# Routed rows fetched as quarter rows and turned by VectorE's block transposes

## Chip, core and metric

The kernel runs on one core of one Trainium2 chip. The metric is the device time of one execution in microseconds (us). Before the change the median of three runs is 294.49 us (294.01 to 295.79).

## What is computed

The input is `x`, 625 rows of 1024 features in float32, with 20000 edges of two types. A graph layer comes first, then a mixture-of-experts layer. Cut to what matters here:

```
g  = x + layernorm(x) + elu(rgcn(t5_norm(layernorm(x)))) @ wo      # graph layer with residual
xf = layernorm(g)                                                  # 625 x 1024, "h2" in the kernel
shared = mean over 2 shared experts of gelu(xf @ sW1 + sb1) @ sW2 + sb2
gates  = xf @ rW + rb                                              # 8 experts
w      = softmax of the two largest gates, zero elsewhere
h_e    = gelu(xf @ W1[e] + b1[e])                                  # 1024 -> 256
moe    = sum over e of w[:, e] * (h_e @ W2[e] + b2[e])             # 256 -> 1024
out = g + xf + shared + moe                                        # residuals as in the reference
```

## The kernel before

The kernel does not run every expert over every row. It routes: each of the 625 rows has two experts, so there are 1250 (row, expert) pairs, and they are packed into 11 tiles of 128 slots (`NJ = 11`). Seven tiles belong wholly to one expert (numbers 4 to 10), three are split into two halves of different experts (0 to 2) and one is split into four quarters (3). The order in which they are worked on is 4, 5, 6, 0, 7, 1, 8, 2, 9, 10, 3.

The stages around the change are these.

- **The normalized rows.** `output_proj` (L976) computes `h2` for each 125-row block, stores it to DRAM as `h2d` from the GpSimd queue (L993), and `to_columns` puts its transpose into `h2T`.
- **Loads.** The SyncE queue loads `w1a` (the eight `W1`, 8 MB, L1078), `sw1` and `w2a` (the eight `W2`, 8 MB, L1109). `w1a` is laid out so that partition p holds the features p, 128 + p, 256 + p and so on.
- **Routing.** `gate` and `route` compute the gates and weights. `slots` (L1188) works out on VectorE, in many small instructions, which slot each pair gets. A matrix product `p_tok` (L1288) turns this into one row number per slot. L1294 makes from it `tok`, the row to gather for each of the 128 x 11 slots; `row` (L1296) says where the result of a slot goes.
- **Shared experts.** `shared_in` (L1170, `p_sh`) runs before, between and after these steps and keeps TensorE filled.
- **Bias rows.** `bias_parts` fetches `b2x` with three DMAs from the GpSimd queue (L641) into a buffer of the pool `io`, which has three buffers; VectorE reads it last at L645 (`b2h`).
- **First half of the routed experts.** For each tile, `fetch` (L1368) gathers the 128 rows with one indirect DMA from the GpSimd queue (L1370) into an `io` buffer `xs`. TensorE transposes them in eight 128 x 128 blocks (L1378, `p_x`). ScalarE copies one half of the result to `xsT` (L1384), VectorE the other (L1382). `xsT` has two buffers. `expert_in` (L1393, `p_h`, L1397) multiplies `xsT` with `w1a`, and VectorE copies the result to `hj` (L1401). `expert_mid` (L1406) transposes `hj` and applies the gelu on ScalarE (L1412, `hjT`). For the halves and quarters of the split tiles ScalarE also copies pieces of `w1a` to `w1m` (L1391). The loop runs the three steps for neighbouring tiles: fetch of step s, `expert_in` of s - 1, `expert_mid` of s - 2.
- **Second half and end.** `p_yj` (L1455) multiplies `hjT` with `w2a`; the rows are scattered to `yt` (L1463), read back as `g` (L1474) and added to `x1` with the shared experts' second product `p_o` (L1510, L1512); the result is stored.

[...] The GpSimd queue of this stage holds, in this order, the three `b2x` DMAs, the eleven gathers and the eleven scatters.

Of the kernel before, what the change touches and what calls it, by code (L numbers as in the profile page):

```python
# [8 lines left out]
F32 = mybir.dt.float32  # L9
F16 = mybir.dt.float16  # L10
BF16 = mybir.dt.bfloat16
F32R = mybir.dt.float32r
I32 = mybir.dt.int32
I16 = mybir.dt.int16
AF = mybir.ActivationFunctionType
ALU = mybir.AluOpType
AX = mybir.AxisListType

N = 625
D = 1024  # L20
# [6 lines left out]
TP = 125  # L27
NT = N // TP
KD = D // 128
# [13 lines left out]
QC = 32  # L43
NJ = 11
# [409 lines left out]
def sparse_kernel(  # L454
# [24 lines left out]
    nc = tc.nc  # L479

    def pool(stack, name, bufs=1, side="left", **kw):
        return stack.enter_context(tc.tile_pool(name=name, bufs=bufs, side=side,
                                                reuse_waits="tile", **kw))

    const = pool(ctx, "const")
# [4 lines left out]
    h2d = dram.tile([N, D], F32, name="h2d")  # L490
# [4 lines left out]
    def ps_acc(name):  # L495
        return psum[0].tile([128, 512], F32, tag="acc", name=name, bufs=nacc[0])

    def ps_mm(name):
        return psum[0].tile([128, 512], F32, tag="mm", name=name, bufs=3)
# [64 lines left out]
    ident = const.tile([128, 128], F32, name="ident")  # L564
# [61 lines left out]
    for i in (2, 3):  # L626
# [5 lines left out]
                                               ap=[[0, 3], [D, NS], [1, D]]))  # L632
    nc.gpsimd.dma_start(bd[:, NS:, :], bass.AP(tensor=b2.tensor, offset=b2.offset,
                                               ap=[[0, 3], [D, NE], [1, D]]))
    b23 = const.tile([3 * QC, D], BF16, name="b23")

    def bias_parts():
# [5 lines left out]
        for j in range(3):  # L643
# [3 lines left out]
            if j < 2:  # L647
# [13 lines left out]
                                    ap=[[0, 4], [D, QC], [1, D]]))  # L661
# [87 lines left out]
    vT = const.tile([128, NV], F32, name="vT")  # L749
# [324 lines left out]
    w1a = pool(in_w, "w1a", side="right").tile([128, NE, KD, H], F32, name="w1a")  # L1074

    def load_w1(es):
        for e in es:
            nc.sync.dma_start(w1a[:, e], W1[e].rearrange("(k p) h -> p k h", p=128))  # L1078

    load_w1(range(2))  # L1080
    sh_in = ExitStack()
    for s in range(NT + 2):
        if s == 0:
# [4 lines left out]
            rt = pool(sh_in, "rt", side="right")  # L1088
# [17 lines left out]
    io = pool(ctx, "io", 3)  # L1106
# [33 lines left out]
    def route():  # L1140
        full = [TP, NT, NE, NE]
        other = gates[:, :, None, :].to_broadcast(full)
        own = gates[:, :, :, None].to_broadcast(full)
        nc.vector.tensor_scalar(lower, lower, 0.0, None, op0=ALU.is_gt)
        above = rt.tile(full, F32, name="above")
        equal = rt.tile(full, F32, name="equal")
        nc.vector.tensor_tensor(above, other, own, op=ALU.is_gt)
        nc.vector.tensor_tensor(equal, other, own, op=ALU.is_equal)
        nc.vector.tensor_mul(equal, equal, lower[:, None, :, :].to_broadcast(full))
        nc.vector.tensor_add(above, above, equal)  # L1150
        cnt = const.tile(wide, F32, name="cnt")
        nc.vector.tensor_reduce(cnt, above, axis=AX.X, op=ALU.add)
        nc.vector.tensor_scalar(sel, cnt, 1.5, None, op0=ALU.is_lt)
        top = const.tile([TP, NT], F32, name="top")
        nc.vector.tensor_reduce(top, gates, axis=AX.X, op=ALU.max)
        ex = const.tile(wide, F32, name="ex")
        nc.vector.tensor_sub(ex, gates, top[:, :, None].to_broadcast(wide))
        nc.scalar.activation(ex, ex, AF.Exp)
        nc.vector.tensor_mul(ex, ex, sel)
        tot = const.tile([TP, NT], F32, name="tot")  # L1160
        nc.vector.tensor_reduce(tot, ex, axis=AX.X, op=ALU.add)
        inv = const.tile([TP, NT], F32, name="tot_inv")
        nc.vector.reciprocal(inv, tot)
        nc.vector.memset(w[:, :, :NS], 1.0)
        nc.vector.tensor_mul(w[:, :, NS:], ex, inv[:, :, None].to_broadcast(wide))


    shT = hid.tile([128, NS, HK, N], F32, name="shT")

    def shared_in(i, t):  # L1170
        b = KD + i * HK + t
        for a, z in CUTS:
            p = ps_acc(f"p_sh_{i}_{t}_{a}")
            for k in range(KD):
                nc.tensor.matmul(p[:, : z - a], sw1[:, i, k, t * 128 : (t + 1) * 128],  # L1175
                                 h2T[:, k, a:z], start=(k == 0), stop=(k == KD - 1))
            nc.scalar.activation(shT[:, i, t, a:z], p[:, : z - a], AF.Gelu, bias=vT[:, b : b + 1])

    wab = const.tile([TP, 2, NT], F32, name="wab")
    tok = const.tile([128, NJ], I32, name="tok")
    row = const.tile([128, NJ], I32, name="row")
    ej = const.tile([1, nt + 4], I32, name="ej")

    def slots():  # L1188
        nc.vector.tensor_scalar(below, below, 0.0, None, op0=ALU.is_gt)
        ones = const.tile([TP, TP], F16, name="ones")  # L1190
        nc.vector.memset(ones, 1.0)
        p = ps_mm("p_rank")
        rank = p[:TP, : NT * NE].rearrange("p (t e) -> p t e", t=NT)
        shared_in(0, 0)
        nc.tensor.matmul(p[:TP, : NT * NE], below, sel.rearrange("p t e -> p (t e)"),
                         start=True, stop=False)
        for t in range(NT - 1):
            nc.tensor.matmul(rank[:, t + 1 :, :], ones,
                             sel[:, t][:, None, :].to_broadcast([TP, NT - 1 - t, NE]),
                             start=False, stop=(t == NT - 2))  # L1200
# [37 lines left out]
        for i in range(2):  # L1238
# [6 lines left out]
                                       op0=ALU.is_ge, op1=ALU.mult)  # L1245
# [12 lines left out]
        full = const.tile([TP, 2, NT], I32, name="full")  # L1258
# [27 lines left out]
        for a in range(2):  # L1286
            for t in range(NT):
                nc.tensor.matmul(q[:, :NJ], oh[:, a, t], oj[:, a, t],  # L1288
                                 start=(a == 0 and t == 0), stop=(a == 1 and t == NT - 1))

        t = rt.tile([128, 2, NJ], F32, name="t")
        nc.vector.tensor_scalar(t[:, 0], q[:, :NJ], float(YB), float(YB), op0=ALU.is_ge, op1=ALU.mult)
        nc.vector.scalar_tensor_tensor(t[:, 1], q[:, :NJ], -1.0, t[:, 0], op0=ALU.add, op1=ALU.subtract)
        named = nc.vector.tensor_scalar(tok, t[:, 1], 0.0, float(N - 1), op0=ALU.max, op1=ALU.min)  # L1294
        nc.vector.tensor_scalar(t[:, 0], q[:, :NJ], 0.5, 4.0 * YB, op0=ALU.is_lt, op1=ALU.mult)
        nc.vector.tensor_tensor(row, t[:, 0], q[:, :NJ], op=ALU.add)  # L1296

        for at in (0, NH2):
            k = kt[:, 0, at : at + NH2]
# [42 lines left out]
    named = slots()  # L1342
    weights_T()
    bias_parts()
    for t in range(HK):
        shared_in(1, t)
    sh_in.close()


# [1 line left out]
    hjT = mid.tile([128, NJ, HK, 128], F32, name="hjT")  # L1351
    xts = ExitStack()
    xt = pool(xts, "xt", 2, side="right")
    _, e_of = nc.values_load_multi_w_load_instructions(
        ej, engines=[mybir.EngineType.PE, mybir.EngineType.Activation], min_val=0, max_val=NE - 1,
        skip_runtime_bounds_check_because="a count of eight ends at most, cut to seven")
# [7 lines left out]
        return ((0, 128, e_of[NH2 + j - 1]),)  # L1364

    xsT, p_hs, w1m = {}, {}, {}

    def fetch(j):  # L1368
        xs = io.tile([128, D], F32, tag="io", name=f"xs_{j}")
        nc.gpsimd.indirect_dma_start(  # L1370
            out=xs, out_offset=None, in_=h2d,
            in_offset=bass.IndirectOffsetOnAxis(ap=tok[:, j : j + 1], axis=0))
        t_ = xt.tile([128, KD, 128], F32, tag="xsT", name=f"xsT_{j}")
        for g in range(2):
            p = ps_acc(f"p_x{g}_{j}")
            for k in range(4):
                at = (4 * g + k) * 128
                nc.tensor.transpose(p[:, k * 128 : (k + 1) * 128], xs[:, at : at + 128], ident)  # L1378
            o = t_[:, 4 * g : 4 * g + 4, :]
            pv = p.rearrange("p (k n) -> p k n", k=4)  # L1380
            if g:
                nc.vector.tensor_copy(o, pv)  # L1382
            else:
                copied = nc.scalar.copy(o, pv)  # L1384
        xsT[j] = t_

        for jj, a, e in copies.get(j, ()):
            w1m[jj, a] = xt.tile([128, 1, KD, H], F32, tag="w1m", bufs=3, name=f"w1m_{jj}_{a}")
            with tc.issue_after(copied.ins):
                for k in range(0, KD, 2):  # L1390
                    nc.scalar.copy(w1m[jj, a][:, :, k : k + 2], w1a[:, bass.ds(e, 1), k : k + 2])  # L1391

# [11 lines left out]
    bT = vT[:, KD + NS * HK :].rearrange("p (e t) -> p e t", t=HK)  # L1404

    def expert_mid(j):  # L1406
        p = ps_mm(f"p_hT_{j}")
        for t in range(HK):
            nc.tensor.transpose(p[:, t * 128 : (t + 1) * 128], p_hs[j][:, t * 128 : (t + 1) * 128], ident)  # L1409
        for t in range(HK):  # L1410
            for a, b, e in parts(j):
                nc.scalar.activation(hjT[:, j, t, a:b], p[:, t * 128 + a : t * 128 + b], AF.Gelu,  # L1412
                                     bias=bT[:, bass.ds(e, 1), t])


    whole = range(NM2, NJ)
# [31 lines left out]
    for n, j in enumerate(ORDER):  # L1448
        y = gat.tile([128, D], F32, tag="y", name=f"ys_{j}")
        for s in range(2):  # L1450
            at = slice(s * 512, (s + 1) * 512)
            p = ps_acc(f"p_yj_{j}_{s}")
            for k in range(HK):
                for a, b, e in parts(j):
                    made = nc.tensor.matmul(p[a:b], hjT[:, j, k, a:b],  # L1455
                                     w2m[j, a, k][:, at] if a else w2a[:, bass.ds(e, 1), k, at],
                                     start=(k == 0), stop=(k == HK - 1))
# [6 lines left out]
            out=yt, out_offset=bass.IndirectOffsetOnAxis(ap=row[:, j : j + 1], axis=0), in_=y, in_offset=None,  # L1464
# [5 lines left out]
    for d in range(NT):  # L1470
        for a in range(2):
            at = a * YB + 1 + d * TP
# [24 lines left out]
    for d in range(NT):  # L1497
# [4 lines left out]
        for at in ((0, 512), (512, D)) if d < NT - 1 else ((0, 512), (512, 768), (768, D)):  # L1502
            n = at[1] - at[0]
            at = slice(*at)
            p = (ps_mm if banks % 8 > 4 else ps_acc)(f"p_o_{d}_{at.start}")
            banks += 1
            with tc.issue_after(made.ins):
                for i in range(NS):
                    for k in range(HK):
                        nc.tensor.matmul(p[:TP, :n], shT[:, i, k, own], sw2[:, i, k, at],  # L1510
                                         start=(i == 0 and k == 0), stop=False)
# [49 lines left out]
```

## Time and profile before

| | us |
|---|---|
| median of three runs | 294.49 |
| profiled execution, its own time | 294.8 |
| its span, first to last instruction | 293.0 |
| TensorE busy | 283.4 |
| VectorE busy | 168.3 |
| ScalarE busy | 103.2 |
| GpSimd busy | 44.1 |
| granted TensorE clock, mean | 0.997 of full |

The span is the time between the first and the last instruction of the profiled execution; 1.8 us of that execution's own time lie outside it. [...]

### The profile page before, as it was taken

The page shows a single profiled execution, that of the slowest core. Times are in us where ns is not written, and L with a number is a line of the kernel's source. Part 1 is how long each engine was busy: PE and PEld are TensorE (multiplying, and loading weights), DVE is VectorE, ACT ScalarE, POOL GpSimd, SP SyncE. Part 2 cuts the span into 40 slices and gives each one's busy share as a digit, 9 for nine tenths or more (in the row PEclk, how much of TensorE's full clock was granted, in tenths as well). Part 3 has the DMA queues.
Part 4 walks back from the last instruction along what each step waited for, and adds up shares of the span by engine and source line. Part 5 has one row for each costly group of instructions (what it writes and reads, how often), then busy time and mean ns, then how long its engine had stood idle before and what let it go on. Part 6 is the DMA issues. An engine that isn't in the chain of part 4 may idle for free.

```text
span 293.0 us, 4532 instructions
## 1 busy us (share of the span) xinstructions
PE 283.4 (97%) x1573; PEld 192.1 (66%) x1573; DVE 168.3 (57%) x459; ACT 103.2 (35%) x237; POOL 44.1 (15%) x101
## 2 busy tenths in 40 slices
PE   7998999999999999899999999999999999999992
PEld 5876777778888555677777987778643334444451
DVE  5699999997874888746925322222134111157920
ACT  2348425513642323353105544656198111000000
POOL 9500000000000024420131312110012223200000
PEclk9999999999999999999999999999999999999998
DMA  6999930000000999999999742420095545389351
GB/s 229 344 322 408 408 117 2 2 1 2 0 0 4 327 364 392 393 392 369 409 353 408 283 143 78 140 74 0 2 342 230 211 194 226 136 332 403 134 156 53
DMA packets 28699, 61.41 MB, mean 210 GB/s; under 512 B 2150, under 2 KB 15981, under 8 KB 28666
## 3 DMA queue, kind: packets, MB, share of 16 engines
q1 hardware_dynamic: 23144, 44.17, 42.0%
q0 software_dynamic: 5232, 16.55, 15.4%
q10 hardware_dynamic: 296, 0.35, 0.5%
q8 instruction: 15, 0.25, 0.3%
q14 instruction: 12, 0.10, 0.1%
HBM read 43.02 MB, written 18.81 MB: 211 GB/s over the span
## 4 chain that ended last, share of the span: by engine, by line
PE 77%; DVE 20%; issue 1%; ACT 1%; ACTq 0%; DVEq 0%
PE p_h L1397 13%; PE p_yj L1455 13%; PE p_o L1510 12%; PE p_sh L1175 11%; PE p_pr L920 9%; PE p_agg L937 5%; PE p_x L1378 3%; DVE ohs L873 3%; DVE ohs L874 2%; PE p_y L983 2%; PE scrap L1000 2%; DVE xh L987 2%; DVE st L776 2%; DVE xh L807 1%; DVE ohk L877 1%; DVE h L747 1%
## 5 line engine op out<-in xcount | busy, mean ns | idle before, releaser
L920 PE MATMUL p_pr<-wg,nT 128*125 128x286 f32 x240 | 61.5, 409 | 1.0 <-ACT nT L825 0.8
L920 PEld LDWEIGHTS p_pr<-wg,nT 128*125 128x125 f32 x240 | 43.8, 187 | 13.2 <-ACT nT L825 1.8
L1397 PE MATMUL p_h<-w1a,xsT 128*128 (+2 forms) x176 | 40.0, 381 | 0.0
L1455 PE MATMUL p_yj<-w2a,hjT 128*128 (+2 forms) x88 | 38.6, 595 | 0.0
L1510 PE MATMUL p_o<-sw,shT 128*125 128x512 f32 (+1 forms) x88 | 36.1, 554 | 0.0
L1175 PE MATMUL p_sh<-h2T,sw 128*128 128x313 f32 (+1 forms) x128 | 35.2, 429 | 0.0
L1397 PEld LDWEIGHTS p_h<-w1a,xsT 128*128 128x128 f32 (+2 forms) x176 | 28.8, 169 | 7.4 <-issue 0.5
L1175 PEld LDWEIGHTS p_sh<-h2T,sw 128*128 128x128 f32 x128 | 23.7, 190 | 8.6 <-issue 0.2
L1455 PEld LDWEIGHTS p_yj<-w2a,hjT 128*128 128x128 f32 (+2 forms) x88 | 14.4, 169 | 22.4 <-issue 22.4
L1510 PEld LDWEIGHTS p_o<-sw,shT 128*125 128x125 f32 x88 | 16.4, 188 | 16.9 <-issue 16.2
L1459 DVE COPY ys<-p_yj 128x512 f32<-128x512 f32 x15 | 10.4, 692 | 28.7 <-PE p_yj L1455 27.0
L1401 DVE COPY hj<-p_h 128x256 f32<-128x256 f32 x11 | 4.7, 425 | 31.1 <-PE p_h L1397 31.1
L994 POOL DMA_DIRECT2D x1d<-xh x10 | 5.3, 531 | 92.4 <-DVE flagf L721 89.0
L983 PE MATMUL p_y<-wo_t,eT 128*125 128x512 f32 (+1 forms) x40 | 18.8, 592 | 0.0
L1463 POOL DMA_INDIRECT yt<-ys,row x11 | 10.8, 981 | 50.5 <-DVE ys L1459 50.5
L1412 ACT ACTIVATE hjT<-p_hT,vT 128x128 f32<-128x128 f32 (+2 forms) x34 | 8.7, 332 | 24.5 <-PE p_hT L1409 24.5
L1486 DVE SCALAR_TENSOR_TENSOR x<-p_o,x 125x512 f32<-125x512 f32 (+1 forms) x11 | 6.9, 639 | 16.3 <-PE p_o L1512 16.3
L1370 POOL DMA_INDIRECT xs<-h2d,tok x11 | 10.4, 948 | 34.5 <-PE p_x L1378 24.9
L937 PE MATMUL p_agg<-P,CT 125*125 125x288 f32 x100 | 15.5, 305 | 0.0
L1397 PE MATMUL p_h<-w1m,xsT 128*64 128x256 f32 (+1 forms) x96 | 14.7, 382 | 0.0
L1455 PE MATMUL p_yj<-w2m,hjT 128*64 128x512 f32 (+1 forms) x48 | 14.1, 595 | 0.0
L1382 DVE COPY xsT<-p_x 128x512 f32<-128x512 f32 x11 | 7.6, 692 | 11.0 <-PE p_x L1378 8.7
(309 smaller groups left out, 422.8 us busy)
## 6 DMA issues: line engine op xcount, KB each, us to landing
w1a<-in_L_ffn_W_dram SPq DMA_DIRECT2D x8, 1024.0 KB
w2a<-in_L_ffn_W_dram SPq DMA_DIRECT2D x8, 1024.0 KB
yt<-zero SPq DMA_DIRECT2D x2, 2560.0 KB
g<-yt SPq DMA_DIRECT2D x10, 512.0 KB
sw<-in_L_ffn_sW_dram SPq DMA_DIRECT2D x4, 1024.0 KB
x<-x1d SPq DMA_DIRECT2D x5, 500.0 KB
x1d<-xh POOLq DMA_DIRECT2D x5, 448.0 KB, 7.2
h2d<-h POOLq DMA_DIRECT2D x5, 448.0 KB, 6.8
```

Source lines behind the costliest of these rows:

```text
L873: nc.vector.tensor_tensor(os, row[:, None].to_broadcast(shape), key, op=ALU.is_equal)
L920: nc.tensor.matmul(p[:TP, :F], nT[:, k, m * TP : (m + 1) * TP], wg[:, k, r, :], start=(k == 0), stop=(k == KD - 1))
L937: nc.tensor.matmul(p[:TP, : F + 2], CT[:, m, at : at + TP], P[:, m, r, i], start=(m == 0 and i == 0), stop=(m == NT - 1 and i == 1))
L983: nc.tensor.matmul(ps[s][:TP, :], eT[:n, k, :], wo_t[:n, k, at], start=(k == 0), stop=False)
L1175: nc.tensor.matmul(p[:, : z - a], sw1[:, i, k, t * 128 : (t + 1) * 128], h2T[:, k, a:z], start=(k == 0), stop=(k == KD - 1))
L1370: nc.gpsimd.indirect_dma_start(out=xs, out_offset=None, in_=h2d, in_offset=bass.IndirectOffsetOnAxis(ap=tok[:, j : j + 1], axis=0))
L1378: nc.tensor.transpose(p[:, k * 128 : (k + 1) * 128], xs[:, at : at + 128], ident)
L1397: nc.tensor.matmul(p[a:b, :H], xsT[j][:, k, a:b], w1m[j, a][:, 0, k, :] if a else w1a[:, bass.ds(e, 1), k, :], start=(k == 0), stop=(k == ...
L1455: made = nc.tensor.matmul(p[a:b], hjT[:, j, k, a:b], w2m[j, a, k][:, at] if a else w2a[:, bass.ds(e, 1), k, at], start=(k == 0), stop=(k = ...
L1459: nc.vector.tensor_copy(y[:, at], p)
L1463: sent.append(nc.gpsimd.indirect_dma_start(out=yt, out_offset=bass.IndirectOffsetOnAxis(ap=row[:, j : j + 1], axis=0), in_=y, in_offset=No ...
L1510: nc.tensor.matmul(p[:TP, :n], shT[:, i, k, own], sw2[:, i, k, at], start=(i == 0 and k == 0), stop=False)
```

## The change

The rows that a tile needs are no longer gathered whole. Each row of `h2d` is seen as four quarter rows of 256 features. Four indirect DMAs per tile, numbered a = 0 to 3, fetch for the slots 32a to 32a + 31 their quarter b into partition 32b + r, r being the slot within its group of 32. A 32 x 32 block transpose within each group of 32 partitions then leaves features on partitions and slots along the free dimension. VectorE does this for the whole tile in one instruction that reads every eighth element. Partition p then holds the features 8p to 8p + 7, and `w1a` is loaded in the same order.

The row numbers for this are made in `slots`: four small matrix products (after `p_tok`) copy the 32 row numbers of group a onto all four groups of partitions, and one VectorE instruction multiplies by four and adds the quarter's number (`quad`). The left operand of those products, `own4`, is made by four ScalarE copies from the identity. TensorE's transposes `p_x` and the two copies of each tile to `xsT` are gone. The `w1m` copies on ScalarE are ordered behind the last gelu issued before them (`turned`), where before they stood behind a copy to `xsT`. `ones`, `above` and `equal` change their buffers so that `own4` fits.

```
-            nc.sync.dma_start(w1a[:, e], W1[e].rearrange("(k p) h -> p k h", p=128))
+            nc.sync.dma_start(w1a[:, e], W1[e].rearrange("(p k) h -> p k h", p=128))
...
-    tok = const.tile([128, NJ], I32, name="tok")
+    tok = const.tile([128, 4, NJ], I32, name="tok")
+    quad = const.tile([128, 1], F32, name="quad")
+    for b in range(4):
+        nc.gpsimd.memset(quad[b * QC : (b + 1) * QC], float(b))
...
-        named = nc.vector.tensor_scalar(tok, t[:, 1], 0.0, float(N - 1), op0=ALU.max, op1=ALU.min)
+        own4 = rt.tile([128, 4, 4, QC], F16, tag="above", name="own4")
+        tf = rt.tile([128, NJ], F16, name="tf")
+        for a in range(4):
+            nc.scalar.copy(own4[:, a], ident[:, None, a * QC : (a + 1) * QC].to_broadcast([128, 4, QC]))
+        nc.vector.tensor_scalar(tf, t[:, 1], 0.0, float(N - 1), op0=ALU.max, op1=ALU.min)
+        q4 = ps_mm("p_tok4")
+        for a in range(4):
+            nc.tensor.matmul(q4[:, a * NJ : (a + 1) * NJ], own4[:, a].rearrange("p b r -> p (b r)"), tf,
+                             start=True, stop=True)
+        named = nc.vector.tensor_scalar(tok.rearrange("p a j -> p (a j)"), q4[:, : 4 * NJ], 4.0, quad,
+                                        op0=ALU.mult, op1=ALU.add)
...
     def fetch(j):
-        xs = io.tile([128, D], F32, tag="io", name=f"xs_{j}")
-        nc.gpsimd.indirect_dma_start(
-            out=xs, out_offset=None, in_=h2d,
-            in_offset=bass.IndirectOffsetOnAxis(ap=tok[:, j : j + 1], axis=0))
+        xs = io.tile([128, 4, D // 4], F32, tag="io", name=f"xs_{j}")
+        for a in range(4):
+            nc.gpsimd.indirect_dma_start(
+                out=xs[:, a], out_offset=None, in_=h2d.rearrange("n (b f) -> (n b) f", b=4),
+                in_offset=bass.IndirectOffsetOnAxis(ap=tok[:, a, j : j + 1], axis=0))
         t_ = xt.tile([128, KD, 128], F32, tag="xsT", name=f"xsT_{j}")
-        for g in range(2):
-            p = ps_acc(f"p_x{g}_{j}")
-            for k in range(4):
-                at = (4 * g + k) * 128
-                nc.tensor.transpose(p[:, k * 128 : (k + 1) * 128], xs[:, at : at + 128], ident)
-            o = t_[:, 4 * g : 4 * g + 4, :]
-            pv = p.rearrange("p (k n) -> p k n", k=4)
-            if g:
-                nc.vector.tensor_copy(o, pv)
-            else:
-                copied = nc.scalar.copy(o, pv)
+        nc.vector.transpose(t_.rearrange("p k (a r) -> p a k r", a=4), xs.rearrange("p a (c k) -> p a k c", k=KD))
...
-            with tc.issue_after(copied.ins):
+            with tc.issue_after(turned[-1].ins):
```

More of the change, by code (lines that the diff above doesn't have):

```diff
@@ L1144, in route @@
         nc.vector.tensor_scalar(lower, lower, 0.0, None, op0=ALU.is_gt)
-        above = rt.tile(full, F32, name="above")
-        equal = rt.tile(full, F32, name="equal")
+        above = rt.tile(full, F32, tag="above", name="above")
+        equal = rt.tile(full, F32, tag="equal", name="equal")
         nc.vector.tensor_tensor(above, other, own, op=ALU.is_gt)
@@ L1176, in shared_in @@
                                  h2T[:, k, a:z], start=(k == 0), stop=(k == KD - 1))
-            nc.scalar.activation(shT[:, i, t, a:z], p[:, : z - a], AF.Gelu, bias=vT[:, b : b + 1])
+            last = nc.scalar.activation(shT[:, i, t, a:z], p[:, : z - a], AF.Gelu, bias=vT[:, b : b + 1])
+        return last
     wab = const.tile([TP, 2, NT], F32, name="wab")
-    tok = const.tile([128, NJ], I32, name="tok")
+    tok = const.tile([128, 4, NJ], I32, name="tok")
+    quad = const.tile([128, 1], F32, name="quad")
+    for b in range(4):
+        nc.gpsimd.memset(quad[b * QC : (b + 1) * QC], float(b))
     row = const.tile([128, NJ], I32, name="row")
@@ L1189, in slots @@
         nc.vector.tensor_scalar(below, below, 0.0, None, op0=ALU.is_gt)
-        ones = const.tile([TP, TP], F16, name="ones")
+        ones = rt.tile([TP, TP], F16, tag="equal", name="ones")
         nc.vector.memset(ones, 1.0)
@@ L1345, in sparse_kernel @@
     for t in range(HK):
-        shared_in(1, t)
+        last_in = shared_in(1, t)
     sh_in.close()
@@ L1366, in sparse_kernel @@
     xsT, p_hs, w1m = {}, {}, {}
+    turned = [last_in]
     def fetch(j):
-        xs = io.tile([128, D], F32, tag="io", name=f"xs_{j}")
-        nc.gpsimd.indirect_dma_start(
-            out=xs, out_offset=None, in_=h2d,
-            in_offset=bass.IndirectOffsetOnAxis(ap=tok[:, j : j + 1], axis=0))
-        t_ = xt.tile([128, KD, 128], F32, tag="xsT", name=f"xsT_{j}")
-        for g in range(2):
-            p = ps_acc(f"p_x{g}_{j}")
-            for k in range(4):
-                at = (4 * g + k) * 128
-                nc.tensor.transpose(p[:, k * 128 : (k + 1) * 128], xs[:, at : at + 128], ident)
-            o = t_[:, 4 * g : 4 * g + 4, :]
-            pv = p.rearrange("p (k n) -> p k n", k=4)
-            if g:
-                nc.vector.tensor_copy(o, pv)
-            else:
-                copied = nc.scalar.copy(o, pv)
+        xs = io.tile([128, 4, D // 4], F32, tag="io", name=f"xs_{j}")
[3 more added lines that the diff above has]
+                in_offset=bass.IndirectOffsetOnAxis(ap=tok[:, a, j : j + 1], axis=0))
+        t_ = xt.tile([128, KD, 128], F32, tag="xsT", name=f"xsT_{j}")
+        nc.vector.transpose(t_.rearrange("p k (a r) -> p a k r", a=4), xs.rearrange("p a (c k) -> p a k c", k=KD))
         xsT[j] = t_
@@ L1411, in expert_mid @@
             for a, b, e in parts(j):
-                nc.scalar.activation(hjT[:, j, t, a:b], p[:, t * 128 + a : t * 128 + b], AF.Gelu,
-                                     bias=bT[:, bass.ds(e, 1), t])
+                turned.append(nc.scalar.activation(hjT[:, j, t, a:b], p[:, t * 128 + a : t * 128 + b],
+                                                   AF.Gelu, bias=bT[:, bass.ds(e, 1), t]))
     whole = range(NM2, NJ)
```

## The prediction

> **What bounds the kernel now.** I read the busy times first, then the chain that ended last in order of time, then GpSimd's and VectorE's instructions in order of time around the change.
>
> ```profile
> PE 283.4 (97%) x1573; PEld 192.1 (66%) x1573; DVE 168.3 (57%) x459; ACT 103.2 (35%) x237; POOL 44.1 (15%) x101
> ```
>
> TensorE is busy for 97% of the span, GpSimd for 15%. So at first sight whatever leaves TensorE is won. The chain (start, length, what) says the same for this stage:
>
> ```profile
> 161.14 1.75 PE p_x L1378 x16
> 162.88 3.46 PE p_h L1397 x16
> 166.34 0.87 PE p_x L1378 x8
> ...
> 203.62 0.87 PE p_x L1378 x8
> 204.49 3.46 PE p_h L1397 x16
> 207.94 0.22 PE p_hT L1409 x2
> 208.16 3.59 PE p_h L1397 x64
> 211.75 0.37 PE p_hT L1409 x2
> ```
>
> It is TensorE without a gap: per tile 0.87 us of transposes, 3.46 to 3.60 of `p_h`, 0.22 to 0.37 of `p_hT`. The last tile's `p_h` starts at 208.16, and from there to the end (`p_yj`, `p_o`) the chain is TensorE again. Nothing behind that point is changed, so the question is when the last `p_h` starts. Last, GpSimd in order of time (start, length, what, idle before it and its releaser):
>
> ```profile
> 145.37 1.49 POOL L641 DMA_DIRECT2D b2x<-bd  x3 [19.25 <-DVE tok L1294]
> 147.18 1.04 POOL L1370 DMA_INDIRECT xs<-h2d,tok  x1 [0.32 <-DVE part L1330]
> 148.52 0.96 POOL L1370 DMA_INDIRECT xs<-h2d,tok  x1 [0.30 <-issue]
> 158.15 0.94 POOL L1370 DMA_INDIRECT xs<-h2d,tok  x1 [8.66 <-DVE b2h L645]
> 162.28 0.94 POOL L1370 DMA_INDIRECT xs<-h2d,tok  x1 [3.20 <-PE p_x L1378]
> 163.53 0.94 POOL L1370 DMA_INDIRECT xs<-h2d,tok  x1 [0.30 <-issue]
> ```
>
> A gather occupies GpSimd for 0.94 us. Where two stand back to back (148.52 and 163.53), the second starts 0.30 us after the first ended, released by nothing but its issue. The pitch of gathers is thus 0.94 + 0.30 = 1.24 us, not 0.94; the first pair, cold, has 1.34. The row at 158.15 shows the third tile's gather waiting for the buffer of `b2x`.
>
> **TensorE.** 88 transposes go: 1.75 for the first two tiles and 0.87 for each of nine more, 9.6 us, all on the chain. Four products for `tok` come, between two `p_sh`: the ten of `p_tok`, of the same kind, took 0.40 us together in TensorE's order of time, so 0.15 for four, and about 0.25 of waiting for `tf`: 0.4. The shared experts then end at 161.5 instead of 161.14. The first block transpose needs their buffers, so it cannot start sooner.
>
> **VectorE.** Per tile one copy of 0.69 goes and one block transpose of 1024 elements per partition comes. There is none in the trace. The nearest row is a float32 operation over as many elements in SBUF:
>
> ```profile
> 153.82 1.22 DVE L648 TENSOR_TENSOR b2x<-b2x,b2h 96x1024 f32<-96x1024 f32 x1
> ```
>
> I take 1.24. Below, nothing excludes the 0.81 us that VectorE needs for the 1024 float32 elements of a one-input operation (L747); above, the stride of eight elements might halve the rate, 2.3. With the `hj` copy (0.43) it is 1.7 us per tile, inside any pitch below, so only the first and last tile's transposes lie on the path. First tile: 161.5 + 0.1 + 1.24 + 0.1 puts the first `p_h` at 162.9, against 162.88: the first 1.75 us are won by TensorE and given back to VectorE.
>
> **ScalarE.** 0.59 us per tile goes; the four copies for `own4` (nearest row: 128 x 128 at 0.33 us, L1412, so 1.3 together) stand where ScalarE idles for 4 us before 139.26. Without that cover they would cost at most those 1.3. The `w1m` copies (4 x 0.64) now stand behind a gelu, two tiles ahead of their use. No cost.
>
> **TensorE's own limit.** From 162.88 to 208.16 are 45.3 us, less nine times 0.87 is 37.5. From 162.9, TensorE alone could start the last `p_h` at 200.4: a gain of 7.8.
>
> **GpSimd.** Eleven gathers become 44. Each still has 128 row numbers, so I keep 0.94 + 0.30. Bounds: 0.94 if the 0.30 hides in a full queue, 1.34 as in the cold pair. Row 163.53, warm and without a wait, is the nearest. Per tile this is 4 x 1.24 = 4.97 us, more than TensorE's 3.7 to 4.0, and more than the 4.5 to 4.8 of a whole tile before. **GpSimd becomes the bound of this stage.**
>
> Its course: `tok` comes about 0.8 us later (146.2), but the `b2x` DMAs keep GpSimd till 146.86, so the first gather starts at 147.2 as before. If the `b2x` DMAs, too, wait for the later `tok`, all gathers slip by up to 0.8; I take 0, as their buffer is cleared earlier. Eight gathers last until 157.2; the ninth, first of tile three, waits for `b2x`'s buffer until 158.15, as now. Then 36 stand without a wait: tile four needs a buffer freed by the first block transpose (162.8) and is due at 163.1; later ones have more room. The last gather starts at 158.15 + 35 x 1.242 = 201.6.
>
> Landing: before it was 4.1 to 4.4 us from issue where no load was running, for 512 KB. A quarter should land sooner:
>
> ```profile
> x1d<-xh POOLq DMA_DIRECT2D x5, 448.0 KB, 7.2
> x1d<-xh POOLq DMA_DIRECT2D x5, 52.0 KB, 6.5
> ```
>
> The last column is us to landing: 0.7 less for 396 KB less. So 3.5. [...]
>
> Sum: 201.6 + 3.5 + 0.2 (the transpose's several semaphores) + 1.24 + 0.1 = 206.65, against 208.16: **1.5 us earlier**. 294.8 (the profiled execution: 293.0 span and 1.8 around it) - 1.5 = 293.3. The runs' median, 294.49, is 0.3 below the profiled one, within their spread.
>
> Pieces of 1 KB become 8 KB in the load of `w1a`. DMA is saturated from 100 to 168, but TensorE is busy 10.00 of 10.00 us in each stretch there, so a sooner end gains nothing; a later one cannot follow from larger pieces.
>
> [...]
>
> ```profile
> 106.01 0.81 DVE L747 TENSOR_SCALAR h<-xh,ln_0m,ln_0ro 125x1024 f32<-125x1024 f32 x1
> 106.39 0.55 POOL L994 DMA_DIRECT2D x1d<-xh  x1 [3.44 <-DVE xh L987]
> ```
>
> The DMA was issued in the middle of such an operation and took 0.55 us, within the 0.52 to 0.56 of all ten. [...]
>
> **Rivals.**
> - *The 0.30 hides, and TensorE stays the bound.* From a pitch of 1.06 down, the last `p_h` is at 200.4: 294.8 - 7.8 = 287.0. For it: TensorE's 97%, and direct DMAs of the same queue stand with no gap (three in 1.49 us). Against it: both back-to-back gathers show 0.30. Chance 0.15.
> - [...] Chance 0.23, with milder prolongations of the pitch from 1.37 on.
> - *GpSimd bounds at about 1.24*, the forecast: chance 0.62. Its own range, pitch 1.17 to 1.33 and the bounds on landing and transpose, is 290 to 297.5; a tenth of a microsecond per gather moves the end by 3.5.
>
> Faster by over 1% needs a pitch below 1.20: the first rival and a part (0.10) of the forecast, 0.25. Slower by over 1%: the second rival and 0.05 of the forecast, 0.28. The rest, 0.47, lies within 1%. The range, 286.8 to 302, takes in the first rival and the lower end of the second.
>
> **What would show it.** GpSimd's gathers 44 times with 0.94 us, 1.24 apart; TensorE idle before `p_h` L1403, about 1 us per tile from the middle of the stage on, released by VectorE's transpose and that by a gather's landing; the last `p_h` near 206.7. Wrong if the pitch is under 1.06 (then no idle time before `p_h`), if a gather beside a transpose takes over 1.1 us, or if the transpose takes more than 3 us.

## The result, and the profile after

The changed kernel took 309.14 us (307.77 to 313.64 over four executions) where the kernel before took 294.44 on the same chip: 1.047 times as long, interval 1.043 to 1.052. (The ratio leaves out the execution of 313.64 us, which lies over 1.5% above the fastest and counts as a slow one.) That is outside the predicted range on the slow side. The profiled execution took 309.28, with a span of 307.4. In three later groups of executions, told below, the same kernel ran on other chips, and there it took about what was predicted. Both results have to be explained.

The page comes first: the row of busy times, and the TensorE clock granted in 40 slices of 7.7 us each.

```profile
PE 282.0 (92%) x1489; PEld 185.0 (60%) x1489; DVE 182.5 (59%) x460; ACT 98.3 (32%) x230; POOL 76.0 (25%) x138
...
PEclk9999999999999999999999966959999999999998
```

TensorE has as much busy time as before (282.0 against 283.4), with 84 fewer instructions: most of the 9.6 us of transposes that went has come back as slower matmuls (all `p_h` together take 63.9 us, for 54.7 before). The clock row shows where: three slices at 0.6, 0.6 and 0.5, between 177 and 208 us of the span. Before, it is 9 in every slice.

The groups of instructions of the changed step, from the same page (busy us and mean ns, then idle time before them and its main releaser):

```profile
L1386 POOL DMA_INDIRECT xs<-h2d,tok x44 | 41.9, 953 | 25.8 <-issue 12.2
...
L1407 DVE COPY hj<-p_h 128x256 f32<-128x256 f32 x11 | 4.6, 422 | 39.2 <-remote 21.0
L1390 DVE STREAM_TRANSPOSE xsT<-xs 128x1024 f32<-128x1024 f32 x11 | 22.3, 2033 | 2.6 <-PE p_sh L1175 2.5
L1418 ACT ACTIVATE hjT<-p_hT,vT 128x128 f32<-128x128 f32 (+2 forms) x34 | 8.8, 332 | 45.0 <-remote 34.2
```

The 44 gathers take what was said, 0.95 us. The block transpose takes 2.03, not 1.24. But the rows that matter are the two with "remote", the profile's word for a wait for which it finds no releaser: the copy `hj` and the gelu `hjT`, which wait for TensorE, have 21.0 and 34.2 us of it. In order of time (start, length, engine, what, idle before it and its releaser):

```profile
171.38 0.44 PE L1415 MATMUL p_hT<-ident,hj 128*128 128x128 f32 x2 [0.50 <-issue]
...
173.30 3.72 PE L1403 MATMUL p_h<-w1a,xsT 128*128 x16 [1.49 <-issue]
...
178.16 0.95 POOL L1386 DMA_INDIRECT xs<-h2d,tok  x1 [0.30 <-issue]
182.23 0.42 DVE L1407 COPY hj<-p_h 128x256 f32<-128x256 f32 x1 [8.98 <-remote]
182.28 0.78 ACT L1418 ACTIVATE hjT<-p_hT,vT 128x128 f32<-128x128 f32 x2 [16.62 <-remote]
...
185.12 0.94 POOL L1386 DMA_INDIRECT xs<-h2d,tok  x1 [6.01 <-DVE xsT L1390]
```

This is how to read it. `p_hT` of the first tile ends at 171.8; its gelu starts at 182.28, 10.5 us later, on a ScalarE that had nothing else to do. The copy at 182.23 is the second tile's, whose `p_h` ended at 170.9, 11.4 us earlier (the row at 173.30 is the third tile's `p_h`). Both start in the same 0.05 us, as if messages from TensorE had been held back and then delivered together. The semaphore events that the trace holds say the same: one of TensorE's is at 161.60, the next ones are at 182.21, 182.25 and 182.41, for work that ended at 170.9, 171.8 and 177.0. Up to 178.16 GpSimd goes on issuing gathers, one every 1.25 us. Then the loop closes: the next block transpose, which VectorE has behind the late `hj` copy, starts only when that has ended (182.81, 0.15 us after it), the `xs` buffer stays full, and GpSimd stops for 6.01 us (and again for 5.04 at 204.87). The chain that ended last shows the same stretch, and what comes after it:

```profile
165.59 5.24 issue
...
173.25 9.00 another core or an unknown queue
182.25 0.42 DVE hj L1407
...
182.81 2.05 DVE xsT L1390
184.86 0.14 issue
184.99 5.78 PE p_h L1403 x32
...
196.69 0.49 issue
197.18 0.38 PE p_h L1403
197.56 1.78 issue
...
223.01 3.59 PE p_h L1403 x64
```

I call such stretches silent: 5.24 us that end at 170.8 (the first tile's `p_h` runs until about 167.3, so 3.6 of them are silent), 9.00 that end at 182.25. In a third, before 202.2, TensorE itself moves by jerks: between the matmuls of one tile stand gaps of 0.49, 1.78 and 0.99 us, and the profile shows nothing that they waited for. So perhaps not only its messages are held back. After the second stretch, the `p_h` of a split tile takes 5.78 us instead of 3.60, at a granted clock of 0.57 of full from 185 to 190, as the table at the end shows. The last `p_h` starts at 223.01, not 206.65.

### The profile page after: what moved, and what is told of

Same layout as the page of the kernel before. It is cut to its first block, busy times and chain, and to the rows that moved or that the text cites. A ratio compares the mean times of both kernels' runs of the same rounds, so it can differ in the third digit from the quotient of the medians.

```text
span 307.4 us, 4405 instructions
## 1 busy us (share of the span) xinstructions
PE 282.0 (92%) x1489; PEld 185.0 (60%) x1489; DVE 182.5 (59%) x460; ACT 98.3 (32%) x230; POOL 76.0 (25%) x138
## 4 chain that ended last, share of the span: by engine, by line
PE 65%; DVE 24%; issue 5%; another core or an unknown queue 3%; ACT 1%; DVEq 0%; ACTq 0%
PE p_yj L1461 12%; PE p_h L1403 11%; PE p_o L1516 11%; PE p_pr L920 9%; PE p_sh L1175 7%; PE p_agg L937 4%; DVE ohs L873 2%; DVE ohs L874 2%; DVE xsT L1390 2%; PE p_y L983 2%; PE scrap L1000 2%; DVE xh L987 2%; DVE st L776 2%; DVE xh L807 1%
## 5 line engine op out<-in xcount | busy, mean ns | idle before, releaser
L1403 PE MATMUL p_h<-w1a,xsT 128*128 (+2 forms) x176 | 44.9, 408 | 9.3 <-issue 5.6
L1386 POOL DMA_INDIRECT xs<-h2d,tok x44 | 41.9, 953 | 25.8 <-issue 12.2
L1403 PEld LDWEIGHTS p_h<-w1a,xsT 128*128 128x128 f32 (+2 forms) x176 | 30.4, 179 | 19.0 <-issue 11.0
L1390 DVE STREAM_TRANSPOSE xsT<-xs 128x1024 f32<-128x1024 f32 x11 | 22.3, 2033 | 2.6 <-PE p_sh L1175 2.5
L1418 ACT ACTIVATE hjT<-p_hT,vT 128x128 f32<-128x128 f32 (+2 forms) x34 | 8.8, 332 | 45.0 <-remote 34.2
L1403 PE MATMUL p_h<-w1m,xsT 128*64 128x256 f32 (+1 forms) x96 | 19.0, 429 | 0.7 <-issue 0.5
```

The costliest lines, as they stand in the source:

```text
L1386: nc.gpsimd.indirect_dma_start(out=xs[:, a], out_offset=None, in_=h2d.rearrange("n (b f) -> (n b) f", b=4), in_offset=bass.IndirectOffsetO ...
L1390: nc.vector.transpose(t_.rearrange("p k (a r) -> p a k r", a=4), xs.rearrange("p a (c k) -> p a k c", k=KD))
L1403: nc.tensor.matmul(p[a:b, :H], xsT[j][:, k, a:b], w1m[j, a][:, 0, k, :] if a else w1a[:, bass.ds(e, 1), k, :], start=(k == 0), stop=(k == ...
L1418: turned.append(nc.scalar.activation(hjT[:, j, t, a:b], p[:, t * 128 + a : t * 128 + b], AF.Gelu, bias=bT[:, bass.ds(e, 1), t]))
```

## Experiments

Theories at first: **A**, the train of 44 gathers holds back TensorE's messages; **B**, the block transposes do; **C**, the new order of the `w1a` load does. The experiments ran in five groups on five chips, here named by their numbers. The chip of the result above, the "first chip", has no number on record; it may be one of the five. "Before" is the kernel before, on the same chip in the same group.

### Chip 5: the parts one by one (one execution each; before 293.94)

`e1_quarters_only` is the kernel before with four quarter-row gathers per tile, whose row numbers four VectorE instructions make; transposes and copies stay.

```
-            out=xs, out_offset=None, in_=h2d,
-            in_offset=bass.IndirectOffsetOnAxis(ap=tok[:, j : j + 1], axis=0))
+        for a in range(4):
+            ... out=xs[:, a * 256 : (a + 1) * 256], in_=h2d.rearrange("n (b f) -> (n b) f", b=4),
+                in_offset=bass.IndirectOffsetOnAxis(ap=tok[:, a, j : j + 1], axis=0))
```

> The kernel before with one part of the change: four gathers of quarter rows per tile, into the same partitions as the whole row had, and TensorE's transposes and the two copies kept. Theory A (a long train of gathers on the GpSimd queue holds back TensorE's semaphore increments, whatever turns the rows): the same silent gaps as after the change, 10 us or more slower than before, about 305 to 312. Theory B (the block transposes of VectorE do it): no such gaps; only the pitch of 1.25 us per gather counts, the last p_h starts near 208, about 294 to 297.

Measured: 296.66. The gathers run at a pitch of 1.25 and the last starts at 201.63, with no silent stretch. Theory A falls, on this chip.

`e2_transposes_only` is the kernel before with whole-row gathers and VectorE's block transpose in place of TensorE's (the rows then stand in the wrong order).

> The kernel before with the other part: one gather of whole rows per tile as before, and VectorE's block transpose in the place of TensorE's transposes and the two copies. The rows are then left in an order that the weights do not match, so this run is for its time alone. Theory A: no gaps, TensorE's own limit with a 2.03 us transpose ahead of the first p_h: about 288. Theory B: gaps as after the change, 300 or more.

Measured: 287.96. No stretch: theory B falls on this chip too, and the 6.0 us gained are those of a stage with TensorE's transposes gone and GpSimd not bounding.

`e3_old_w1_order` is the changed kernel with the load back in the old order, `e4_two_buffers` the changed kernel with `pool(ctx, "io", 2)` for 3.

> The changed kernel with w1a loaded in the order of before, in 1 KB pieces (so the features do not match the turned rows; for its time alone). Theories A and B: as the changed kernel, 307 to 311. Theory C (the 8 KB pieces of the load, or how w1a then lies, disturb the stage): back under 300.

> The changed kernel with two buffers for the gathered rows where it has three: a tile's four gathers wait for the block transpose two tiles earlier, so that the trains of gathers are cut to four to eight. Theory A: the gaps go or shrink although GpSimd does the same work later: 295 to 303. Theory B: no better than the changed kernel, 309 or more, because each gather now waits longer.

Measured: 293.57 and 298.82. In `e3` there is no stretch and the last `p_h` starts at 206.9; that seemed to speak for C. In `e4`, which has the new order, there is no long stretch either; its block transposes wait 24.2 us for landings, since a tile's gathers cannot run ahead. Taken together these four did not settle it.

### Chip 2: the order of the load (before 294.8)

`e5_small_pieces` splits each load of `w1a` so that the values land as in the change but in the old pieces of 1 KB. `e6_before_new_order` and `e7_quarters_new_order` are the kernel before and `e1` with the changed load line alone.

```
-            nc.sync.dma_start(w1a[:, e], W1[e].rearrange("(p k) h -> p k h", p=128))
+            for o in range(2):
+                nc.sync.dma_start(w1a[:, e, o::2], W1[e].rearrange("(p k) h -> p k h", p=128)[:, o::2])
```

> The changed kernel with each expert's w1a load split into two transfers, one of the even and one of the odd k, so that every value lands where the change puts it but in pieces of 1 KB as before the change. Nothing else differs. Theory C1 (the size of the pieces is what disturbs the stage): no silent stretches on TensorE, last p_h near 207, 293 to 294.5 us. Theory C2 (the stretches come of how the train of gathers happens to lie against TensorE's instructions, and the order of the load only shifted it): anything between 293 and 310, with stretches at other places or none. Theory C3 (the contents of the tiles, the order of features, matter): as the change, 308 to 310.

> The kernel before with the load of w1a alone in the order of the change, so in pieces of 8 KB; TensorE's transposes and whole-row gathers stay, and the features of rows and weights no longer match, so that only its time is read. Theory C1: if the pieces alone do it, silent stretches here too and some 300 us or more. Theory C2, and the prediction's step that costs the load at nothing: 293.5 to 295.

> The kernel before with four quarter-row gathers for each tile (on the same partitions, TensorE's transposes stay) and the load of w1a in pieces of 8 KB; features of rows and weights do not match, so that only its time is read. With the old load it took 296.7 us. Theory C1: silent stretches, 305 us or more. Theory C2: 296 to 297.5 without stretches, or with some if the train happens to lie so.

`e8_three_whole` is `e5` with three tiles fetched whole, by one gather with the row numbers from before the quartering (`tokw`), and transposed by TensorE:

```
+    WHOLE = (tiles[0], tiles[5], tiles[-1])
...
+        if j in WHOLE:
...
+            xv = xs.rearrange("p a (c k) -> p k (a c)", k=KD)
...
+                    nc.tensor.transpose(p[:, k * 128 : (k + 1) * 128], xv[:, 4 * g + k], ident)
```

> A version meant to beat both: as e5_small_pieces, but three of the eleven tiles (the first, the sixth and the last) are fetched as whole rows and transposed by TensorE with a stride of eight columns. 35 gathers at 1.25 us instead of 44: the train ends 11 us earlier, so TensorE, with 24 transposes (2.6 us) more than the change, sets the pace: last p_h near 203, 289 to 291 us. Theory C1: that. Theory C2: that, or more by the length of any silent stretch.

Measured: `e5` 309.09, `e6` 295.03 (ratio 1.001, interval 0.998 to 1.004), `e7` 309.79 (1.054, 1.048 to 1.060), `e8` 304.26 (1.035, 1.028 to 1.043). The waits of the stage in `e7`, then in `e6` (who waited for whom, total us, times, longest):

```profile
DVE hj L1404 <- remote: 21.0, 2, 13.0
ACT hjT L1415 <- remote: 13.8, 2, 6.9
```

```profile
DVE hj L1401 <- PE p_h L1397: 31.2, 11, 3.4
POOL xs L1370 <- PE p_x L1378: 23.9, 7, 3.9
ACT hjT L1412 <- PE p_hT L1409: 20.7, 9, 3.7
```

The two differ in the gathers alone, four of quarter rows for one of a whole row (and in the few VectorE instructions that number the quarters, long done by then). `e6` has its waits on named TensorE instructions, `e7` has the silent ones, without a single block transpose in it. So on this chip the train of small gathers makes the stretches, and the block transposes are not needed for them (B). The load's new order alone does not make them (`e6`), and the size of its pieces does not matter (`e5`). Whether the new order has a part in it together with the train was not tested: no kernel with small gathers and the old order ran on a chip that shows stretches. What theory A did not explain is why `e1` on chip 5, the same gathers with the old order, has nothing of the sort.

### Chip 9: the same kernel again (before 294.24)

> The changed kernel once more, beside e9_old_order_again on one chip. Theory A (a train of small gathers holds back TensorE, whatever the order of the load; the looks without silent stretches were on a chip that is quicker at this): like its neighbour, both 308 to 311 us or both 293 to 297. Theory C (the order of the load decides): 308 to 311 beside 293.6.

> The changed kernel with w1a in the order of before, as e3_old_w1_order; the features of rows and weights do not match, so that only its time is read. Theory A: like e9_after_again. Theory C: 293 to 295 while e9_after_again takes 308 to 311.

Measured: the unchanged file of the change takes 294.42 (292.49 to 295.51, ten executions), a ratio of 1.000 (0.997 to 1.003); with the old load order 294.01. So the new order does not bring the stretches to this chip (C), and the 309 is gone with both. The waits of the stage in `e9_after_again`:

```profile
ACT hjT L1418 <- PE p_hT L1415: 24.7, 9, 7.1
DVE xsT L1390 <- DMA xs<-h2d,tok: 11.8, 5, 2.7
POOL xs L1386 <- issue: 10.1, 33, 0.3
DVE hj L1407 <- PE p_h L1403: 8.4, 5, 3.6
```

Nothing is remote; the block transposes wait for landings, as forecast. The end of the stage in order of time, and the end of its chain:

```profile
194.76 2.04 DVE L1390 STREAM_TRANSPOSE xsT<-xs 128x1024 f32<-128x1024 f32 x1 [2.75 <-DMA xs<-h2d,tok]
195.69 0.94 POOL L1386 DMA_INDIRECT xs<-h2d,tok  x1 [0.30 <-DMA xs<-h2d,tok]
...
196.94 3.69 PE L1403 MATMUL p_h<-w1a,xsT 128*128 x16 [1.05 <-DVE xsT L1390]
```

```profile
200.69 0.95 POOL xs L1386
201.94 2.67 DMA xs<-h2d,tok
204.74 2.04 DVE xsT L1390
206.91 3.66 PE p_h L1403 x64
```

GpSimd, landing (the row with DMA), VectorE, TensorE: the chain that the prediction drew, with 206.91 at its end for 206.65.

`e10_halves` has two gathers of half rows (512 features) per tile, with row numbers to match, `e11_paced` six small memsets after each gather.

```
-        for a in range(4):
+        for a in range(2):
...
```
```
+            for _ in range(6):
+                nc.gpsimd.memset(quad, 0.0)
```

> The changed kernel with two gathers of half rows for each tile in place of four of quarter rows, on the partitions of whole rows, so that rows come out in the wrong order and only the time is read: 22 gathers with pieces of 2 KB, the same bytes, block transposes kept. Theory A with the number of gathers as what counts: no silent stretches, GpSimd needs 2.5 us a tile and bounds nothing, TensorE's own pace holds, 287 to 289 us. Theory B (the block transposes hold TensorE back): still stretches, over 295.

> The changed kernel with six small memsets by GpSimd (about 0.1 us each) after every gather: the train has the same 44 gathers and bytes but a pitch of about 1.9 us instead of 1.25. If the density of the train is what holds TensorE back, the waits put down to something remote go, and the stage follows GpSimd: the train ends near 231, last p_h near 237, 318 to 324 us in all. If each gather holds TensorE back by its own share, the stretches stay and the time is 330 or more.

Measured: `e10` 288.39 (0.977, 0.971 to 0.983). Its last `p_h` starts at 201.38, and the wait has turned round: GpSimd now waits 12.0 us for block transposes. So on a chip without stretches the number of gathers is what costs the change its gain, and TensorE's own limit is about where the prediction put it (200.4). `e11` took 333.09. By its number that fits the second case, but no wait of the stage is remote, and it tells nothing about the theories: the memsets mostly did not come between the gathers. Single ones, of 0.11 or 0.12 us, hide in the 0.30 between two of them, so that the pitch there stays 1.25, and the others stand in lumps, one of 65 memsets and 10.1 us; and on this chip there was no stretch to cure.

### Chips 1 and 14: which kind of chip, and a better version

> e8_three_whole once more, beside the changed kernel on one chip. If the changed kernel runs without silent stretches there (293 to 295), this takes 289 to 291 by the sum given before: 35 gathers, TensorE sets the pace. If the changed kernel has its stretches (308 to 310), this has them too: some 304.

> e10_halves once more (rows come out in the wrong order, only its time is read). Where the changed kernel has stretches: if it is the number of gathers in a train that holds TensorE back, 22 with waits between them give none or short ones, 287 to 292; if the block transposes have a part in it, 295 or more. Where the changed kernel has none: 287 to 289.

> e2_transposes_only once more (whole-row gathers, block transposes by VectorE, rows in the wrong order, only its time is read). 11 gathers: 287 to 289 on either kind of chip, if the block transposes alone hold nothing back; over 295 where the changed kernel has stretches, if they do.

> The changed kernel for the third time. By now 308 to 310 without a partner of its kind, and 293 to 295 as e9_after_again on another chip. Theory D (the chip decides whether a train of gathers holds TensorE back): one of the two again, the same in all its executions, and the other quarter-row kernel of this call (e13) on the same side. If instead the executions of one chip fall on both sides, it is chance of the moment and not the chip.

Measured on chip 1 (before 294.43): `e13` 289.2 (0.981, 0.977 to 0.985), `e14` 288.55, `e15` 288.03, and the changed kernel, `e16`, 293.84 (0.998, 0.995 to 1.000).

> The changed kernel for the fourth time, as the mark of the kind of chip: 293 to 295, or 308 to 310 with silent stretches. Theory D: all executions of this call on one side.

> e10_halves once more (rows in the wrong order, only its time is read). Beside a changed kernel of 308 to 310: 287 to 292 if the number of gathers is what holds TensorE back, 295 or more if block transposes or the bytes gathered do. Beside one of 293 to 295: 288 to 289 again.

Measured on chip 14 (before 294.19): the changed kernel 294.72 (1.000, 0.996 to 1.004), halves 288.14. No stretch on either chip, so whether 22 gathers or block transposes beside whole rows are safe on a chip like 2 was not measured.

| kernel | first chip | 2 | 5 | 9 | 1 | 14 |
|---|---|---|---|---|---|---|
| before | 294.44 | 294.8 | 293.94 | 294.24 | 294.43 | 294.19 |
| the change (on 2: `e5`; on 5: `e3`) | 309.14 | 309.09 | 293.57 | 294.42 | 293.84 | 294.72 |
| quarters, TensorE's transposes (on 2: `e7`, new load order; on 5: `e1`, old) | | 309.79 | 296.66 | | | |
| three tiles whole | | 304.26 | | | 289.2 | |

`e13` beats both kernels on chip 1, and by the sum written down beforehand (289 to 291). Its chain shows why: TensorE's work stands in it nearly without a gap.

```profile
190.24 3.63 PE p_h L1422 x32
193.87 0.02 issue
193.89 0.44 DVE hj L1426
194.32 0.09 issue
194.41 4.22 DMA xs<-h2d,tokw
198.63 0.04 issue
198.68 1.16 PE p_x L1397 x8
199.84 3.46 PE p_h L1422 x16
203.29 0.22 PE p_hT L1434 x2
203.51 3.59 PE p_h L1422 x64
```

The one gap that costs TensorE anything here is 0.80 us before the row at 198.68: it waits for the last, whole-row gather, which lands 4.22 us after it starts. The last `p_h` starts at 203.51, 4.7 before that of the kernel before. On chip 2 the same file takes 304.26 and loses to it.

## Why the prediction was wrong, and what of it held

**The step that failed** is a wait that the prediction put at nothing. Its sum allows 0.1 us where one engine hands over to the next, and 0.2 from the last landing to the transpose; the end of the chain on chip 9, shown above, has 0.13 in both places. On the first chip hand-overs from TensorE took 3.6 us (the first tile's `p_h` to its copy), 11.4 (the second tile's) and 10.5 (the first tile's `p_hT` to its gelu). The prediction, and every rival in it, took for granted that an engine learns of a result when it is there; it had no term for messages that come late. With that, two of its terms fell:

- "Then 36 stand without a wait", under "GpSimd". The gathers waited twice for block transposes, 6.01 and 5.04 us, which stood behind `hj` copies that had not heard from TensorE. (Before that, the ninth gather got the buffer of `b2x` at 159.40, not at 158.15.) The last gather started at 213.6 instead of 201.6. On chip 9 the last `p_h` starts 4.97 us after the last gather (201.94 and 206.91), so my estimate is that this alone puts it at 218.6.
- "TensorE's own limit" of 37.5 us from the first `p_h` to the last. It took 59.3 us (163.70 to 223.01), with waits, gaps and half clock in it. From 184.99 on, the chain that ended last holds no gather, only TensorE. So on this chip TensorE, and not GpSimd, sets the start of the last `p_h`: 223.01.

**What is shown of the cause.** With the gathers alone changed, chip 2 shows the stretches (`e7`) or does not (`e6`). The very same kernel took 292 to 296 us in 30 of 30 executions on chips 9, 1 and 14 and 307.8 or more in all four on the first; on chip 2 all twelve executions of the three kernels with many small gathers were long. In no group did executions of one kernel fall on both sides. So it takes both: a train of small gathers, and a chip, or a condition of it for a time, that can't bear it. These two weren't told apart, as no numbered chip was used twice. That the new load order is needed as a third thing isn't excluded, as said under chip 2: every run with stretches had it.

**What stays open** is what holds TensorE's messages back. The traces give hints. The trace of the result holds 2917 semaphore events (an event records that an engine or a DMA has reported something done), that of `e9_after_again` 3540, from the same program. What is missing is mostly the gathers' landings: each of the eight semaphores that count them has 99 to 130 events instead of 178 or 179. The traces of `e5`, `e7` and `e8` are short in the same way (2947 to 3117).

A missing event is not a missing message. On the first chip VectorE has no event between 163.66 and 182.67, and yet TensorE started at 171.38 on what VectorE finished at 171.32 (`hj`), and at 173.30 on what it finished at 173.25 (the transpose). TensorE's own messages do come late, and the two longest waits end just after the landings stop: its events at 182.21 and 202.20 follow last landings at 180.81 and 201.46, those of `e7` at 174.58 and 204.48 follow landings at 173.85 and 204.35. (Shorter waits, to 170.9 and 193.6, ended while landings went on.) So a path for these events or their records, filled by the landings, that loses some and holds TensorE up for others, would fit; it is my guess, and no trace shows such a path. Every time here comes from a recorded execution, so no run separates the kernel from its recording. This cause is argued, not shown.

**The half clock** (granted 0.50) came after the silent stretches, so I take it as their consequence; the order in time is all that speaks for it. It cost 2.2 us where it was seen whole (5.78 for 3.60).

**Point by point, on the chips without stretches:**
- The pitch of 1.24 us per gather: measured 1.25 (0.95 + 0.30), also beside block transposes. It decides the stage, as said. The last gather starts at 201.94, 202.64 and 202.83 on chips 9, 1 and 14, for 201.6.
- The landing was taken as 3.5; measured 2.8, median of 41 gathers on chip 9. I stood too near the old row, 4.4. The 0.7 us that I took off rest on the two `x1d` rows; the `h2d` rows of the same list show 6.8 us for 448 and for 52 KB alike.
- The block transpose was taken as 1.24; measured 2.03, near the upper bound of 2.3. The nearest row, a float32 operation over as many elements with two inputs, was the wrong neighbour: 1024 elements took 2.5 times as long as the 1024 elements of a one-input operation (L747, 0.81). How much of that is the stride's was not shown: no kernel has a block transpose without the stride. The two errors, -0.7 and +0.8, cancel, so that 206.91 for 206.65 is partly luck. And the gain of 1.5 us itself can't be seen in the times: the ratios are 1.000, 0.998 and 1.000.
- TensorE idles about 1 us per tile: as said, but on chip 9 only before the last four of eleven tiles (1.00, 1.05, 1.02 and 1.13 us), not from the middle on.
- The load in pieces of 8 KB costs nothing: 294.42 against 294.01 on chip 9, 295.03 against 294.8 on chip 2. (That TensorE was busy for all of each stretch from 100 on was misread: from 100 to 130 it is 29.09 of 30.00 us. Nothing came of it.)
- The first rival's place for TensorE's limit, 287.0 in all: `e10`, in which GpSimd bounds nothing, took 288.4, 288.6 and 288.1.
- The second rival, gathers prolonged by block transposes, with its chance of 0.23 and the upper end of the range: no run shows such a term. The row at 195.69 has one beside a block transpose: 0.94; on the first chip every gather after 159 took 0.94 or 0.95 us. The DMA that the prediction shows beside L747 took 0.55. But beside another VectorE instruction gathers did take longer, see below.

So the forecast of 293.3, "no change", describes the kernel on chips 9, 1 and 14, and it fails on the first, by 15.8 us.

## What to carry to other kernels

Where a gather occupies GpSimd as long whatever its piece, look to fewer, larger ones before saving a transpose: count the gathers at their pitch (here, for 128 row numbers, 0.94 us and a gap of 0.30 with whole and half rows, 0.95 and 0.30 with quarter rows), and spread them only so far that TensorE stays the bound, as the version with three whole-row tiles does. Before believing a small gain from a design with long trains of small DMAs, time it on several chips: here kernels with quarter rows ran as summed on four of the five numbered chips, and some 15 us longer on the fifth and in the first result. A wait "remote" on two engines that ended in the same instant (182.23 and 182.28), with the producer done for 11.4 and 10.5 us, pointed here away from the schedule and at how the message travels.

## What the runs showed of the hardware

- A 32 x 32 block transpose of 128 x 1024 float32 on VectorE, read with a stride of eight elements, took 2.01 to 2.08 us in the profiles of the result, `e5`, `e8`, `e9_after_again`, `e10` and `e11`.
- Gathers that GpSimd started beside VectorE's two-input operation L648 took 1.70 to 1.75 us on chips 9, 1 and 14 instead of 0.95. In `e9_after_again`:

```profile
153.59 1.22 DVE L648 TENSOR_TENSOR b2x<-b2x,b2h 96x1024 f32<-96x1024 f32 x1
...
153.98 1.75 POOL L1386 DMA_INDIRECT xs<-h2d,tok  x1 [0.30 <-issue]
```

L648 ends at 154.81, 0.83 after the gather began; the gather takes 0.80 more than its usual 0.95. The same pair two microseconds later does the same (a gather at 156.03 that takes 1.75, beside L648 from 155.63 to 156.85). On the first chip, where a gather began 0.25 before L648, it took only 1.02. So by these rows it is the start of a gather that is held. By what, no run shows; the block transposes did nothing of the kind.
- TensorE's clock fell after a silent stretch. In windows of 5 us (us, then busy us and counts of PE, PEld, DVE, ACT, POOL, then the granted clock, DMA share, GB/s) of the first chip:

```profile
175.00:180.00 5.00, 2.02 (x10) 1.44 (x8) 0.00 (x0) 0.00 (x0) 3.19 (x4) 0.91 0.34 102
180.00:185.00 5.00, 0.69 (x3) 0.33 (x4) 2.61 (x3) 2.68 (x6) 0.00 (x0) 0.50 0.06 21
185.00:190.00 5.00, 5.00 (x28) 3.18 (x30) 2.10 (x2) 0.64 (x3) 3.79 (x4) 0.57 0.27 79
190.00:195.00 5.00, 5.00 (x30) 3.88 (x28) 2.38 (x2) 1.34 (x4) 3.78 (x4) 1.00 0.36 105
```

TensorE was busy for 2.71 of the 10 us to 185; the granted clock was 0.50 from 180 to 185, and 0.57 in the 5 us after it had work again.
